# Four graph layers on one core: half of a diagonal block by transposition, row work on ScalarE, shared pair buffers

## Chip, core and metric

The kernel runs on one core of one Trainium2 chip. The metric is the device time of one execution in microseconds (us); several executions are timed and their median is given. The engines are TensorE (PE, matmuls; PEld is its weight load), VectorE (DVE), ScalarE (ACT), GpSimd (POOL) and SyncE (SP), which issues the large transfers. [...]

## What is computed

There are 4096 nodes with 64 features each, `x` (4096 x 64), and one dense matrix `adj` (4096 x 4096). About one entry in 256 of `adj` is nonzero, but the kernel treats it as dense. Four layers follow each other; each takes h = relu(layernorm(x)) and adds its result to x:

```
L0: relu((adj @ h) @ W.T + b)
L1: q, k, h1 = lorentz_linear(...)       # three small linear maps, normalised by row
    att = adj * sigmoid(a * (q . k) + b) ; support = att @ h1
    support / sqrt(|inner(support)|)
L2: log_ij = logmap(h_i, h_j)            # needs acosh-like logarithms for all pairs i, j
    agg_i = sum_j adj_ij / deg_i * log_ij ; expmap(agg @ W + b)
L3: rank of each nonzero of a row (running count), weight 2**-(distance from the last), at most 100;
    out = w @ (h @ W) + b
```

Layer 2's pair value depends on a distance that is the same for (i, j) and (j, i). What differs is only the factor `adj_ij` or `adj_ji`.

## The kernel before, in words

Sources stand on the 128 partitions, targets in the free dimension. The targets are cut into 8 blocks of 512 (`W`, `NB`), the sources into 16 groups of 256 (`NG`, two chunks of 128 each, `G = 2`). A tile of work is thus 128 partitions x 2 chunks x 512 targets, that is 128 x 1024, with the matching piece of the transposed `adj` (512 KB) loaded for it by `feed`.

**Order of work.** The kernel is written as many small generators (one for each step of each layer, such as `l1_sigmoids` or `l2_clamps`), each of which yields the engine it needs next and the time from which it can go. `in_turn` (line 702) picks the next step each time by a cost estimate (`Pace`, line 58: estimated durations and one DMA load per 1.45 us) and so fixes every engine's queue when the program is built. Nothing is decided at run time: a wait in a queue holds all that stands behind it on that engine. Work by row (layernorms, small maps, normalisations: 512 rows at a time) runs in `tail` entries started by `follow`; at most two of those are in progress. They, layer 2's transposes and layer 3's counts share two PSUM banks (`spare`, line 331). `after0` to `after3` finish a layer for a block of rows, `before0` to `before3` prepare the next layer for it.

**Layer 0** (`l0_sums`): PE sums `adj` times `h` per target block. The degrees (row sums of `adj`) are added up on DVE in `degree_sums` (line 835) into a `dg` tile; `LEFT` (line 28) names four source groups of each block whose degrees are left for layer 1 (line 802), except for the last block.

**Layer 1** (`l1_atts`, `l1_sigmoids`, `l1_weights`, `l1_sums`): two matmuls give the scores `mm` in a pair tile of PSUM (two such tiles), ACT takes the sigmoid into one of six `sig` buffers (`SIG`), DVE multiplies by `adj`, PE sums. When a block's last sum is done, `after1` and then `before2` run for it: copies and squares on DVE and ACT, small vectors on DVE, a power on POOL, and four transposes through PE whose results ACT copies into `RT`, `LT`, `RB` and `LB`.

**Layer 2** uses the symmetry. Items (`work`, line 943) are taken for target block i and source block j from i on, two items (halves) for each (i, j): 16 diagonal items with i = j, 56 with i < j (`two`). Each item is worked as follows: distances on PE (`l2_dists`), Square on ACT, clamp on DVE, signs on PE (`l2_signs`), Ln and two Exp on ACT (`l2_roots`), `t<-mm,t` on DVE (`l2_coshs`), Ln on ACT, `t<-t,v` on DVE (`l2_pairs`), `w<-t,adj` on DVE (`l2_weights`), a sum on PE. For `two` items the pair values are also turned by eight PE transposes (`l2_turns`), multiplied by a second `adj` tile (`l2_weights2`, `w<-tr,adj`), summed (`l2_sums2`) and gathered in `others`. `in_steps` (line 1156) fixes the relative order of the steps per engine. `v` and `t` have three buffers each in a pool that is opened in `second_part` (line 956), when layer 1's last sum is done and its buffers are closed; `second_part` also loads the Ln/Exp table on ACT and writes `fars` (a constant of layer 3, 128 x 4096) on DVE.

**Layer 3**: a mask on DVE, counts on PE (`l3_counts`: `tr<-...,pick`, a copy `total` on DVE, `tr<-total,spread`, a copy `chunks` on DVE), ranks on PE (`l3_ranks`, two pair tiles), the weight `wt` on ACT, sums on PE (`l3_sum`). `l3_ranks` issues a pair of ranks and then one or two sums that are possible.

In the profile all instructions have the line of the helper that records them (L128), so they are told apart by the names of their tiles.

Of the kernel before, what the change touches and what calls it, by code (L numbers as in the profile page):

```python
# [9 lines left out]
F32 = mybir.dt.float32  # L10
# [3 lines left out]
AF = mybir.ActivationFunctionType  # L14
# [29 lines left out]
EPS = 0.01  # L44
TURN = "PE"
# [12 lines left out]
class Pace:  # L58
# [56 lines left out]
    def load(self, t):  # L115
        self.free["DMA"] = max(self.free["DMA"], self.now) + 1.45
        self.ready[self.name(t)] = self.free["DMA"] + 2.0
# [18 lines left out]
def kernel(ctx: ExitStack, tc: tile.TileContext, a: dict, out: bass.AP):  # L136
# [313 lines left out]
    def before2(ib, st):  # L450
        rb, lb = rbs[slot["now"]], lbs[slot["now"]]
        h = rt("h", [P, CB, D])
        yield from layernorm_relu(ib, h)
        sq = rt("r_sq", [P, CB, D])
        DVE.tensor_mul(sq, h, h)
# [20 lines left out]
        for k in range(2):  # L476
            DVE.tensor_mul(hh[:, :, k, :], h, ic.to_broadcast([P, CB, D]))
        DVE.tensor_copy(HA[:, cs(ib), 0:D], hh[:, :, 0, :])
        l = rt("l2", [P, CB, D])
        DVE.tensor_scalar(l, hh[:, :, 0, :], -2.0 * SC, None, ALU.mult)  # L480
        yield from transposed(hh.rearrange("p c k d -> p c (k d)"), P, RT[:, ws(ib)])

# [83 lines left out]
    def after1(ib, acc, st):  # L566
        e = rows.tile([P, W], F32, tag="e", name="e")
        DVE.tensor_copy(e, acc)
# [13 lines left out]
        if dg is not None:  # L582
            st["dg_free"][ib % 2] = pace.latest
        yield ON_V
        if dg is not None:
            DVE.tensor_add(
                deg[:, cs(ib), :], deg[:, cs(ib), :], ps[:, n : n + CB].unsqueeze(2)
            )
        s = rt("h", [P, CB, D])
        DVE.tensor_copy(s, v)  # L590
        sq = rt("r_sq", [P, CB, D])
        DVE.tensor_mul(sq, s, s)
# [109 lines left out]
    def in_turn(threads):  # L702
# [5 lines left out]
        while waiting or tail:  # L708
            best = None
            for k, entry in enumerate(tail):  # L710
                if k < 2 or entry["evicts"]:
                    need = entry["need"]() if entry["need"] else 0.0
                    if need is None or (entry["on"] == TURN and not spare):
                        continue
                    start = max(entry["at"], pace.free[entry["on"]], need)
                    if best is None or start < best[0]:
                        best = start, entry
            for thread in waiting:
                on, need = thread[1]
                t = need()  # L720
                if t is not None and (best is None or max(t, pace.free[on]) < best[0] - EPS):
                    best = max(t, pace.free[on]), thread
            pace.now, what = best
            if what in tail:
                advance(what)
                continue
            pace.latest = 0.0
            what[1] = next(what[0], None)
            if what[1] is None:
                waiting.remove(what)  # L730
# [58 lines left out]

    early = ExitStack()  # L790
# [10 lines left out]
    def group(layer, ib, g):  # L801
        degree = (g in LEFT and ib < NB - 1) == (layer == 1)
# [97 lines left out]
    def l1_sigmoids():  # L900
        for n, d in enumerate(l1):
# [3 lines left out]
            d["att"] = w01.tile([P, G, W], F32, tag="sig", name="sig", bufs=SIG)  # L905
# [10 lines left out]
    def l1_sums():  # L916
        for pair in pairs:
# [6 lines left out]
            if d["last"]:  # L924
                ib = d["ib"]
                follow(with_mark(2, ib, after1(ib, acc, st), before2(ib, st)), ON_V, evicts=True)
# [18 lines left out]
         "last": j == NB - 1 and s == CB // G - 1, "two": i < j, "left": 1, "at": 0.0}  # L945
        for i in range(NB) for j in range(i, NB) for s in range(CB // G)
    ]
    twos = [d for d in work if d["two"]]

# [6 lines left out]
    def second_part():  # L956
# [12 lines left out]
        log_exp_tables()  # L969
# [4 lines left out]
    def wt(name, **kw):  # L974
        return w2["pool"].tile([P, G, W], F32, tag=name, name=name, **kw)

    def l2_dists():
        for d in work:
# [3 lines left out]
            pair_tile(d)  # L982
            for c in range(G):
                b = slice(c * D, (c + 1) * D)
                PE.matmul(
                    d["ps"][:, c, :], LT[b, d["g"], :], RT[b, ws(d["ib"])],
                    start=True, stop=False,
                )
            for c in range(G):
                b = slice(2 * c * Q, (2 * c + 1) * Q)  # L990
                PE.matmul(
                    d["ps"][:, c, :], LB[b, d["g"], :], RB[b, ws(d["ib"])],
                    start=False, stop=True,
# [3 lines left out]
    def l2_squares():  # L997
        for k, d in enumerate(work):
            yield "ACT", lambda: latest(
                opened.get("second"), d.get("dist"), ago(work, k, 3, "paired")  # L1000
            )
            d["v"] = wt("v", bufs=3)
            ACT.activation(d["v"], d["ps"], AF.Square)
            d["square"] = pace.latest

    def l2_clamps():
        for d in work:
            yield "DVE", lambda: d.get("square")
            DVE.tensor_scalar(d["v"], d["v"], -half, V_MIN, ALU.add, ALU.max)
            d["clamped"] = pace.latest  # L1010

    def l2_signs():
        for d in work:
            yield "PE", lambda: d.get("square")
            for c in range(G):
                b = slice((2 * c + 1) * Q, (2 * c + 1) * Q + 2)
                PE.matmul(
                    d["ps"][:, c, :], LB[b, d["g"], :], RB[b, ws(d["ib"])],
# [4 lines left out]
    def l2_roots():  # L1023
        for k, d in enumerate(work):
            yield "ACT", lambda: latest(
                d.get("clamped"), ago(work, k, 3, "weighed"), ago(work, k, 3, "turned")
            )
            d["t"] = wt("t", bufs=3)
            ACT.activation(d["v"], d["v"], AF.Ln)
            ACT.activation(d["t"], d["v"], AF.Exp, scale=0.5)  # L1030
            d["root"] = pace.latest
            ACT.activation(d["v"], d["v"], AF.Exp, scale=-0.5)
            d["inverse"] = pace.latest

    def l2_coshs():
        for d in work:
            yield "DVE", lambda: latest(d.get("root"), d.get("signed"))
            DVE.scalar_tensor_tensor(d["t"], d["ps"], 0.5 * SC, d["t"], ALU.max, ALU.add)
            d["read"] = pace.latest

    def l2_logs():
        for d in work:
            yield "ACT", lambda: d.get("read")
            ACT.activation(d["t"], d["t"], AF.Ln, scale=2.0 / SC)
            d["log"] = pace.latest

    def l2_pairs():
        for d in work:
            yield "DVE", lambda: latest(d.get("log"), d.get("inverse"))
            DVE.scalar_tensor_tensor(d["t"], d["t"], top, d["v"], ALU.min, ALU.mult)  # L1050
            d["paired"] = pace.latest

    def l2_weights():
        for k, d in enumerate(work):
            yield "DVE", lambda: latest(d.get("paired"), arrival(d), ago(work, k, 2, "summed"))
            d["w"] = wt("w")
            DVE.tensor_mul(d["w"], d["t"], d["adj"])
# [3 lines left out]
    def l2_turns():  # L1061
        for d in work:
            for c in range(G if d["two"] else 0):
                yield "PE", lambda: d.get("paired") if spare else None
                d["tr", c] = ps = bank()
                for k in range(CB):
                    b = slice(k * P, (k + 1) * P)
                    PE.transpose(ps[:, b], d["t"][:, c, b], ident)
            d["turned"] = pace.latest
            if not d["two"]:  # L1070
# [17 lines left out]
    def l2_weights2():  # L1088
        for k, d in enumerate(twos):
            for c in range(G):  # L1090
# [177 lines left out]
    def l3_ranks():  # L1268


        for n, pair in enumerate(pairs3):
            yield "PE", lambda: latest(
                ready(pair[0]["chunks"]) if "chunks" in pair[0] else None, pair_tiles_free(),
                work[-1].get("dist"),
            )
            chunks = []
            for d in pair:
                pair_tile(d)
                for c in range(G):
                    chunks.append((d["g"] * G + c, d["ps"][:, c, :]))  # L1280
                    PE.matmul(
                        d["ps"][:, c, :], near, d["m"][:, c, :], start=True,
                        stop=chunks[-1][0] == NC - 1, skip_group_check=True,
                    )
            for q, (c, rank) in enumerate(chunks):
                b = slice(q * Q, (q + 1) * Q)
                if c < NC - 1:
                    PE.matmul(
                        rank, late["fars"][b, c, :], pair[0]["chunks"][b, :], start=False,
                        stop=True, skip_group_check=True,  # L1290
                    )
            for d in pair:
                d["ranked"] = pace.latest
            for _ in range(1 + n % 2):
                t = sum_need()
                if sums3 and t is not None:
# [30 lines left out]
    def l3_sum():  # L1327
# [22 lines left out]
        if d["last"]:  # L1350
# [5 lines left out]
        feed(order, "early"), feed(order23, "second"), second_part(), third_part(), l2_loads2(),  # L1356
# [8 lines left out]
            (l2_coshs(), 0, once), (l2_weights2(), 1, if_two(2)),  # L1365
        ),
        l2_gathers(), l3_weights(), l3_ranks(), l3_counts(), l3_masks(),
# [47 lines left out]
```

## Time and profile before

| | |
|---|---|
| three runs | 1213.37, 1216.04, 1216.13 us; median 1216.04 |
| profiled execution | 1215.13 us, its span 1213.4 us, 15538 instructions |
| busy | PE 1085.3 (89%), DVE 980.9 (81%), ACT 797.6 (66%), POOL 114.7 (9%) |
| mean granted PE clock | 0.971 |
| adj transfers | 512 of 512 KB, 271.75 MB in all, mean 224 GB/s |

The rows of the page read: engine, operation, output<-inputs, shape, count | busy us in total, mean ns of one | idle time of that engine just before, and what ended it. Stretches of the span are given from its start.

### The profile page before, as it was taken

The numbers are of one execution on the slowest core, as the hardware profiler recorded it, in microseconds if no ns is written. First come the engines' busy times: TensorE is split into PE (matmuls) and PEld (weight loads), VectorE is DVE, ScalarE is ACT, GpSimd is POOL, SyncE is SP. The second block draws the span as 40 slices with busy tenths as digits, with TensorE's granted clock in tenths as the row PEclk, the third lists the DMA queues.
The fourth block names the chain that finished last, engine by engine and source line by source line (L and its number), as shares of the span: only waits on it lengthen the run. The fifth ranks groups of instructions, "written<-read, shape, count | busy, mean of one in ns | idle before, by whom it ended". The sixth has DMA issues, their size and how long they took to land.

```text
span 1213.4 us, 15538 instructions
## 1 busy us (share of the span) xinstructions
PE 1085.3 (89%) x5368; PEld 443.9 (37%) x5368; DVE 980.9 (81%) x1621; ACT 797.6 (66%) x1204; POOL 114.7 (9%) x99
## 2 busy tenths in 40 slices
PE   4799999998999999689989979989888779999998
PEld 1244443333333333234434434444333323333333
DVE  6788789879999998779989999999989984554551
ACT  1055546666656666589898888888877775555554
POOL 2222212101101010000010010000100120000000
PEclk9899999999999999799999999989989899999999
DMA  8899999864767765335534534444444489888830
GB/s 300 326 393 373 366 362 331 328 234 141 266 227 242 250 230 181 122 120 191 178 125 160 197 105 168 145 139 156 140 156 156 144 311 361 305 306 305 300 110 9
DMA packets 77190, 271.75 MB, mean 224 GB/s; under 512 B 10040, under 2 KB 11064, under 8 KB 77112
## 3 DMA queue, kind: packets, MB, share of 16 engines
q1 hardware_dynamic: 75456, 270.57, 62.7%
q8 instruction: 42, 0.69, 0.2%
q10 hardware_dynamic: 1656, 0.20, 0.1%
q14 instruction: 36, 0.29, 0.1%
HBM read 269.68 MB, written 1.05 MB: 223 GB/s over the span
## 4 chain that ended last, share of the span: by engine, by line
PE 48%; DVE 24%; ACT 13%; issue 7%; DMA 5%; POOL 3%; ACTq 0%; SPq 0%; DVEq 0%; POOLq 0%
PE acc L128 25%; PE mm L128 15%; PE tr L128 9%; DMA adj<-in_adjT_dram 4%; DVE w L128 4%; DVE t L128 4%; ACT wt L128 4%; DVE dg L128 3%; DVE sig L128 2%; ACT v L128 2%; ACT sig L128 2%; POOL lo_s L128 2%; ACT t L128 1%; ACT lo_sq L128 1%; DVE v L128 1%
## 5 line engine op out<-in xcount | busy, mean ns | idle before, releaser
L128 PE MATMUL acc<-w,HA 128*65 128x256 f32 (+1 forms) x736 | 258.6, 488 | 20.9 <-DVE w L128 11.7
L128 ACT ACTIVATE sig<-mm,att_b,att_a 128x1024 f32<-128x1024 f32 x128 | 148.4, 1200 | 83.6 <-PE mm L128 74.8
L128 ACT ACTIVATE v<-v 128x1024 f32<-128x1024 f32 x144 | 152.1, 1057 | 47.6 <-DVE v L128 45.0
L128 ACT ACTIVATE wt<-mm 128x1024 uint16<-128x1024 f32 x124 | 120.2, 1021 | 96.1 <-PE mm L128 96.1
L128 DVE TENSOR_TENSOR sig<-sig,adj 128x1024 f32<-128x1024 f32 x128 | 151.9, 1220 | 11.1 <-ACT sig L128 10.8
L128 PE MATMUL acc<-adj,HA 128*64 128x512 f32 x512 | 127.7, 629 | 23.2 <-DVE HA L128 22.4
L128 DVE TENSOR_TENSOR dg<-dg,adj 128x1024 f32<-128x1024 f32 x113 | 137.9, 1221 | 3.4 <-DMA adj<-in_adjT_dram 2.1
L128 PE MATMUL mm<-qT,kT 64*128 64x512 f32 x512 | 131.7, 623 | 8.8 <-ACT sig L128 8.6
L128 PEld LDWEIGHTS acc<-w,HA 128*65 128x65 f32 x736 | 96.8, 142 | 112.2 <-issue 64.6
L128 PE MATMUL acc<-sig,HL 128*64 128x512 f32 x512 | 122.5, 603 | 0.8 <-DVE sig L128 0.8
L128 PE MATMUL acc<-wt,S 128*64 128x512 bf16 x496 | 99.6, 390 | 0.2 <-ACT wt L128 0.2
L128 DVE SCALAR_TENSOR_TENSOR t<-t,v 128x1024 f32<-128x1024 f32 x72 | 89.7, 1246 | 9.8 <-ACT t L128 9.8
L128 DVE SCALAR_TENSOR_TENSOR t<-mm,t 128x1024 f32<-128x1024 f32 x72 | 87.6, 1217 | 4.5 <-PE mm L128 4.2
L128 PE MATMUL mm<-RT,LT 64*128 64x512 f32 x288 | 82.6, 651 | 7.2 <-DVE t L128 7.0
L128 DVE TENSOR_TENSOR w<-t,adj 128x1024 f32<-128x1024 f32 x72 | 87.8, 1220 | 1.4
L128 ACT ACTIVATE t<-t 128x1024 f32<-128x1024 f32 x72 | 75.5, 1049 | 9.4 <-DVE t L128 9.4
L128 DVE TENSOR_TENSOR w<-tr,adj 128x512 f32<-128x512 f32 x112 | 73.2, 684 | 9.9 <-PE tr L128 9.9
L128 DVE TENSOR_SCALAR RT<-adj 128x1024 bf16<-128x1024 f32 x74 | 49.7, 690 | 37.0 <-PE mm L128 36.5
L128 ACT ACTIVATE t<-v 128x1024 f32<-128x1024 f32 x72 | 76.1, 1057 | 2.3
L128 PEld LDWEIGHTS mm<-qT,kT 64*128 64x128 f32 x512 | 42.4, 185 | 86.1 <-ACT sig L128 49.0
L128 ACT ACTIVATE v<-mm 128x1024 f32<-128x1024 f32 x72 | 72.6, 1008 | 1.6 <-PE acc L128 1.6
L128 PE MATMUL tr<-ident,t 128*128 128x128 f32 x448 | 61.0, 279 | 7.7 <-DVE t L128 4.4
(201 smaller groups left out, 1301.3 us busy)
## 6 DMA issues: line engine op xcount, KB each, us to landing
adj<-in_adjT_dram SPq DMA_DIRECT2D x512, 512.0 KB, 4.7
x<-in_x_dram SPq DMA_DIRECT2D x4, 256.0 KB, 4.1
out_dram<-h SPq DMA_DIRECT2D x8, 128.0 KB, 2.9
b<-in_b_dram ACTq DMA_DIRECT2D x2, 32.0 KB, 6.5
W<-in_W_dram ACTq DMA_DIRECT2D x3, 16.0 KB, 4.0
W0T<-in_W0T_dram ACTq DMA_DIRECT2D x2, 16.0 KB, 5.4
W1T<-in_W1T_dram ACTq DMA_DIRECT2D x1, 16.0 KB, 5.2
W1T<-in_b_dram ACTq DMA_DIRECT2D x1, 0.2 KB
```

The lines of the kernel that those rows point to most:

```text
L128: done = self.tc.keep_in_program_order(getattr(self.engine, op)(*args, **kw))
```

## The change

- **Cut items.** The second item of each diagonal block (`cut`) is worked only for the block's last 256 targets; all its steps run on 128 x 2 x 256. For its first 256 targets, the pair values of the first item (sources 0 to 255, targets 256 to 511) are turned by four PE transposes in a spare bank and multiplied by `adj` in one more DVE instruction.
- **Rows on ScalarE.** In `after1` and `before2` the copies, squares and scalings of one operand go from DVE to ACT: `e`, `h`, two `r_sq`, the second half of `r` (`hh`), the copy to `HA`, `l`; a small copy `r_c` is new.
- **Pair buffers.** One pool of six buffers serves `sig` in layer 1 and `v` and `t` in layer 2. The first squares need only the buffers of layer 1's older groups, not the end of layer 1. The table load is put right after layer 1's last sigmoid (`second_tables`).
- **Rows wait at the hand-over.** From the table load until item 4 (`FIRST`) is weighed, `in_turn` sets the row steps back by 0.02 us of planned time, so that layer 2's own steps go first where both could.
- **Degrees.** Block 0's four left degree groups go back to layer 0.
- **Layer 3.** While a pair of ranks can't be issued in the plan, sums that can are issued ahead of it (`l3_pass`).
- **Planner.** A load is planned at 1.37 us, not 1.45.

```diff
     def load(self, t):
-        self.free["DMA"] = max(self.free["DMA"], self.now) + 1.45
+        self.free["DMA"] = max(self.free["DMA"], self.now) + 1.37
...
     (before2)
+        yield ON_S
         sq = rt("r_sq", [P, CB, D])
-        DVE.tensor_mul(sq, h, h)
+        ACT.activation(sq, h, AF.Square)
+        yield ON_V
...
-        for k in range(2):
-            DVE.tensor_mul(hh[:, :, k, :], h, ic.to_broadcast([P, CB, D]))
-        DVE.tensor_copy(HA[:, cs(ib), 0:D], hh[:, :, 0, :])
+        DVE.tensor_mul(hh[:, :, 0, :], h, ic.to_broadcast([P, CB, D]))
+        yield ON_S
+        ACT.copy(hh[:, :, 1, :], hh[:, :, 0, :])
+        ACT.copy(HA[:, cs(ib), 0:D], hh[:, :, 0, :])
         l = rt("l2", [P, CB, D])
-        DVE.tensor_scalar(l, hh[:, :, 0, :], -2.0 * SC, None, ALU.mult)
+        ACT.activation(l, hh[:, :, 0, :], AF.Copy, scale=-2.0 * SC)
...
     (after1)
-        DVE.tensor_copy(e, acc)
+        ACT.copy(e, acc)
...
+        yield ON_S
+        s = rt("h", [P, CB, D])
+        ACT.copy(s, v)
+        sq = rt("r_sq", [P, CB, D])
+        ACT.activation(sq, v, AF.Square)
...
     (in_turn)
+                    if "tables" in opened and "weighed" not in work[FIRST]:
+                        start += 2 * EPS
...
+    pairp = ctx.enter_context(tc.tile_pool(name="pairs", bufs=SIG))
+    def pair_buffer(name):
+        return pairp.tile([P, G, W], F32, tag="pair", name=name)
...
-        degree = (g in LEFT and ib < NB - 1) == (layer == 1)
+        degree = (g in LEFT and 0 < ib < NB - 1) == (layer == 1)
...
+    OWN = G * P
+    def part(d, t):
+        return t[:, :, OWN:] if d["cut"] else t
+    def targets(d):
+        return slice(d["ib"] * W + (OWN if d["cut"] else 0), (d["ib"] + 1) * W)
...
+    def second_tables():
+        yield "ACT", lambda: l1[-1].get("read")
+        log_exp_tables()
+        opened["tables"] = pace.free["ACT"]
...
     (l2_squares)
-                opened.get("second"), d.get("dist"), ago(work, k, 3, "paired")
+                d.get("dist"), l1[2 * k - SIG].get("summed") if 2 * k < SIG else 0.0,
+                ago(work, k, SIG // 2, "paired"),
...
     (l2_turns)
+            if d["first"]:
+                yield "PE", lambda: d.get("paired") if spare else None
+                d["tr", 0] = ps = bank()
+                for k in range(CB):
+                    b, c = slice(OWN + k // G * P, OWN + (k // G + 1) * P), k % G
+                    PE.transpose(ps[:, k * P : (k + 1) * P], d["t"][:, c, b], ident)
...
     (l2_weights2)
+                own["w"] = w2["pool"].tile([P, G, W], F32, tag="w", name="w")
+                DVE.tensor_mul(
+                    own["w"][:, :, 0:OWN], d["tr", 0].rearrange("p (k j) -> p k j", j=OWN),
+                    own["adj"][:, :, 0:OWN],
+                )
...
     (l3_pass, was l3_ranks)
+            while rank_need(pair) is None:
+                yield "PE", lambda: first_of(rank_need(pair), sum_need() if sums3 else None)
+                if rank_need(pair) is None:
+                    l3_sum()
+            yield "PE", lambda: rank_need(pair)
+            l3_rank(pair)
```

## Prediction

> **What bounds the kernel now.** I read the page's engine shares first (PE 89%, DVE 81%, ACT 66%). Those are means over four layers, so I cut the span into stretches. The columns are length, then busy time (and instructions) of PE, PEld, DVE, ACT and POOL, granted clock, DMA share and GB/s:
>
> ```profile
> 0.00:50.00 50.00, 27.56 (x95) 7.77 (x96) 33.80 (x82) 5.30 (x11) 13.21 (x35) 0.90 0.82 303
> 50.00:230.00 180.00, 171.48 (x889) 73.72 (x890) 156.99 (x239) 94.68 (x321) 42.07 (x22) 1.00 0.97 368
> 230.00:487.00 257.00, 244.25 (x1112) 88.44 (x1108) 229.19 (x475) 162.31 (x284) 26.89 (x16) 1.00 0.66 222
> 487.00:532.00 45.00, 29.68 (x116) 11.44 (x112) 31.66 (x66) 28.54 (x45) 2.32 (x2) 0.77 0.27 94
> 532.00:605.00 73.00, 72.89 (x345) 34.94 (x344) 68.47 (x78) 66.55 (x70) 0.00 (x0) 1.00 0.54 182
> 605.00:975.00 370.00, 324.11 (x1468) 150.88 (x1466) 343.86 (x488) 309.23 (x336) 24.11 (x19) 0.95 0.44 149
> 975.00:1004.00 29.00, 23.05 (x130) 7.98 (x130) 24.56 (x56) 20.72 (x28) 6.08 (x5) 0.94 0.94 355
> 1004.00:1206.00 202.00, 189.23 (x1214) 67.15 (x1210) 91.23 (x141) 109.58 (x114) 0.00 (x0) 1.00 0.68 248
> ```
>
> To be seen: layer 0 (to 230) runs at DMA's rate with a nearly full PE; layer 1 (230 to 487) at PE's; at 487 to 532 no engine is full, that is the hand-over to layer 2; layer 2's plain stretch (532 to 605) is PE's, 5.85 us an item, with 0.4 us of DVE slack in each; 605 to 975 holds the diagonal blocks and rows, PE loses 46 us and DVE is nearly gapless; layer 3 is PE's, with 12.8 us lost.
>
> Second, the timeline around 487, where the hand-over is lost:
>
> ```profile
> 486.50 1.23 DVE L128 TENSOR_TENSOR sig<-sig,adj 128x1024 f32<-128x1024 f32 x1 [1.43 <-ACT sig L128]
> 491.20 1.02 ACT L128 ACTIVATE v<-mm 128x1024 f32<-128x1024 f32 x1 [1.58 <-PE acc L128]
> 496.76 1.06 ACT L128 ACTIVATE v<-v 128x1024 f32<-128x1024 f32 x1 [4.54 <-DVE v L128]
> 500.70 2.08 PE L128 MATMUL mm<-RT,LT 64*128 64x512 f32 x4 [7.01 <-DVE t L128]
> 507.53 3.68 PE L128 MATMUL acc<-w,HA 128*65 128x512 f32 x4 [4.20 <-DVE w L128]
> 530.93 1.23 DVE L128 TENSOR_TENSOR w<-t,adj 128x1024 f32<-128x1024 f32 x1
> ```
>
> The first square of layer 2 waits until layer 1's last sum is done (its buffers lie where layer 1's lay); then its clamp stands in DVE's queue behind `fars` and block 7's rows. The last line is the weighing of item 3. Third, groups by form and waits, for prices:
>
> ```profile
> L128 DVE SCALAR_TENSOR_TENSOR t<-mm,t 128x1024 f32<-128x1024 f32 x72 | 87.6, 1217 | 4.5 <-PE mm L128 4.2 <-ACT t L128 0.2
> L128 DVE TENSOR_TENSOR w<-tr,adj 128x512 f32<-128x512 f32 x112 | 73.2, 684 | 9.9 <-PE tr L128 9.9
> L128 DVE TENSOR_SCALAR v<-v 128x1024 f32<-128x1024 f32 x72 | 49.3, 684 | 2.3 <-ACT v L128 2.3
> PE mm L128 <- ACT sig L128: 8.6, 17, 1.2
> PE tr L128 <- DVE total L128: 6.1, 8, 0.8
> PE mm L128 <- ACT wt L128: 3.4, 13, 0.3
> ```
>
> The last three are layer 1's and layer 3's PE waits (total, times, longest).
>
> **The change, part by part.** All sums are against the profiled execution: 1215.1 us, its span 1213.4.
>
> *Cut items.* Eight second diagonal items become half as wide. Off DVE, each: clamp 0.68 to about 0.35, cosh and pair product 1.22 and 1.25 to 0.68 each (the 512-wide row). The weighing of 1.22 becomes two of 0.68. Net 3.15+1.22 against 1.71+1.36: 1.3 us saved. ACT saves five times 0.43 (1.057 to 0.63, on the line between 0.414 at 256 wide, `r_sq<-ln_xc`, and 1.057 at 1024), 2.1 us. PE saves about half a `mm<-RT,LT` group (0.5 us of 1.13) and pays four transposes (0.6): nothing. The new wait: the second weighing waits for those transposes and a spare bank; behind it on DVE stand the next clamp and pair product. The nearest row, `w<-tr`, waited 9.9 us over 29 of 112, 0.1 us each; at most the 0.4 us of its worst. For the seven blocks in the DVE-bound stretch 605 to 1000: 7 x 1.3 = 9, of which I take 8, because six times (10.8 us) PE waited there for `ACT v`. Ends 4 and 10.
>
> *Rows on ScalarE.* Per block off DVE (start to start, block 7's timeline): `e` 0.61, `h` 0.45, two `r_sq` 0.91, second `r` 0.34, `HA` and `l` 0.20 each: 2.7 us. On to ACT: 0.58 + 0.37 + 2 x 0.41 + 3 x 0.40 + 0.2, about 3.2 us. [...] (`S<-hb` 0.399 on ACT, `HA<-r` 0.28, 0.20 start to start, on DVE). Counted in engine time the move loses 0.5 us a block, 4 us. Counted by what bounds, it pays: in layer 1 ACT has 95 us idle of 257.
>
> In layer 1, seven blocks x 2.7 and the degree sums of block 0 (copy, three adds, half add: 4.6) take some 23 us off DVE. PE is the bound there and can gain no more than its idle 12.8. DVE is gapless from 267 to 310, and in 275 to 300 PE loses 4.3. Elsewhere PE is sent two score groups in a row because weights are late, and waits for a pair tile (8.6 in 17 waits). In the changed program's order such doubles fall from 17 to 10: 8.6 x 7/17 = 3.5, partly the same time as the 4.3. I take 5; ends 1 and 8.
>
> *Degree sums into layer 0.* Four adds of 1.22, 4.9 us of DVE before 50, where it has 16 us idle; they stand ahead of the half add of `dg` (44.4, now about 49.5), which PE's transposes need at 49.7. The order puts two more `acc<-adj` matmuls ahead of them. If DVE's room fails, four buffers come free later and DMA-bound layer 0 slips. I take 0; ends -1 (gain) and +2.
>
> *Hand-over.* In the changed program the first square follows the last sigmoid on ACT, its clamp the last `sig` product on DVE; `fars` follows, rows come after item 3. From the shown anchor (last `sig` product ending 487.7): square ends 487.5; clamp 488.4; `fars` 490.6; the table load (1.28 in the trace) ends about 489; Ln and two Exp to 492.3; cosh 492.5; Ln 493.8; pair product 495.1; first weights 496.3, against 507.5. Item 1 is half, its weights done by 499.4; item 2 about 505.7; item 3 at 510.8 against 532.1. That is 21 us earlier, but before had done block 7's rows by then. Those now cost DVE 12.5 - 2.7, some 9.5 us, among items with 0.4 us slack each, so over six items 7 us come back. ACT holds 3.2 + 4.7 us of row work there against 0.75 slack an item. I allow 3 more for ACT standing in its queue for PE (`LB` waited 4.19 at 528). 21 - 7 - 3 = 11; ends 5 and 14.
>
> The clock: in the trace the 7.0 us PE gap is followed by a group at 2.08 instead of 1.13 and sums at 3.68 instead of 1.93. [...] by the row alone a shorter gap might keep the clock and give some 2 us more. [...] no gain from the clock, inside the upper end.
>
> *Table load.* Earlier by its place in the queue, same number (19); counted above. [...] The trace has 488.33 + 1.28, nothing following, so I keep 1.28.
>
> *Layer 3.* A sum may now go while ranks wait. In the old order 9 of 16 `tr<-total` groups follow directly on counting (`pick`) and wait for its copy, in the new 13 of 16 follow a sum of 1.5 us, longer than the 0.8 it hides. So the 6.1 go, 5.5 to be careful; the 3.4 stay. Ends 2 and 7.
>
> *At no cost:* the pair buffers in layer 2 (three `v` and three `t` as before, strictly in turn), the planner's load price and delay of rows (order only).
>
> Sum: 5 + 11 + 8 + 5.5 + 0 = 29.5. 1215.1 - 29.5 = 1185.6, say 1186; the runs' median of 1216.0 is 0.9 above the profiled one, which is within their spread, so it is left.
>
> **The rivals.** (a) *The hand-over only shifts the rows* (0.25). DVE, ACT and PE are all near 5.1 to 5.85 us an item, so 9.5 us of deferred rows come back in full and queueing eats more: 5 there, 2 in layer 1, 6 at the diagonals, 5 in layer 3: 18, 1197. For it: ACT is 91% busy in 532 to 605. Against: before idles DVE 13 us here.
> (b) *Everything lands at its good end* (0.15): 8 + 13 + 9 + 6 = 36 and up, 1178. For it: DVE's gaplessness at 900 to 1000, where each us saved is a us.
> (c) *Slower* (0.03): ScalarE's in-order queue. Each block has gained four round trips between DVE, ACT and PE; if row copies wait there for transposes as `LB` did (4.19, with DVE's `t` idle 4.82 behind it), all five activations stand. It decides from 29.5 / 8 = 3.7 us a block; at 4.5 it costs 36: 1222. Against: ACT's rows waits in layer 1 sum to 17 us over seven blocks, and PE did not wait on most.
> (d) *It does not do what it says* (0.02): halves cost what wholes do and rows only move: within 0.3%, 1215. The 512-wide rows speak against it.
>
> **Numbers.** Main case 0.55 at 1186, 1181 to 1192. The range takes (a) and (b) with their spread: 1175 to 1201. A measurement tells about 0.3% apart; faster by more 0.95, within 0.02, slower 0.03.
>
> **What will show it.** First `acc<-w` some 6 us after the end of layer 1's last sum instead of 16; item 3 weighed near 21 us earlier against that sum; `PE tr <- DVE total` near 1; half-wide `v`, `t` forms at 0.35, 0.68 and 0.63; layer 1's `PE mm <- ACT sig` about 5. Wrong if ACT waits for PE transposes by several us a block, or if 605 to 975 keeps its length because PE, not DVE, sets it.

## The result and the profile after

The changed kernel takes 1198.38 us (median of four runs, 1195.06 to 1202.06), the kernel before 1214.7 in the same comparison: 0.986 of the time, with a 95% interval of 0.983 to 0.988. The forecast was 1186 with a range of 1175 to 1201. The time lies in the range, near rival (a)'s 1197 and not in the main case: some 16 to 19 us were gained where 29.5 were summed. Rival (a)'s total is met and its terms are not (5, 2, 6 and 5 for hand-over, layer 1, diagonals and layer 3, against 9.0, 4.7, 4.3 and 0.9 in the table below), so that the total came out near it is luck.

The profiled execution after took 1196.08 us, span 1194.4, clock 0.978: 19.0 less than the profiled one before. I cut it near the same places of the work (columns: length, then busy time and instructions of PE, PEld, DVE, ACT, POOL, granted clock, DMA share, GB/s):

```profile
230.00:483.00 253.00, 247.04 (x1106) 88.78 (x1104) 208.41 (x421) 178.31 (x336) 25.47 (x16) 0.99 0.68 225
483.00:510.00 27.00, 21.34 (x88) 7.90 (x87) 20.56 (x28) 24.43 (x30) 0.95 (x1) 0.87 0.48 164
986.00:1189.00 203.00, 190.59 (x1195) 69.33 (x1215) 92.31 (x143) 111.84 (x117) 0.00 (x0) 1.00 0.68 246
```

The hand-over row (the second) is 27 us where it was 45, but the block's rows are now behind it. The stretch to dwell on is the one with the diagonal blocks. From the end of the 16th weighing (`w<-t,adj`, the last of the first block row) to layer 2's last sum, before (first line) and after:

```profile
600.64:977.08 376.44, 330.40 (x1492) 153.49 (x1489) 349.77 (x498) 314.58 (x340) 24.11 (x19) 0.95 0.44 149
586.89:959.00 372.11, 325.99 (x1518) 153.90 (x1517) 340.69 (x500) 297.77 (x338) 26.20 (x18) 0.97 0.44 150
```

DVE has lost 9.1 us of work, as sized (7 x 1.3), and the stretch only 4.3. From milestone to milestone of the two traces:

| stretch | before | after | gain | forecast |
|---|---|---|---|---|
| start to the end of the last `sig` product | 487.73 | 483.04 | 4.7 | 5 |
| from there to the 16th `w<-t,adj` (the first block row) | 112.9 | 103.9 | 9.0 | 11 |
| from there to layer 2's last sum | 376.5 | 372.1 | 4.3 | 8 |
| from there to layer 3's last sum | 231.1 | 230.1 | 0.9 | 5.5 |

The timeline of the hand-over in the changed kernel shows that part as it was drawn up. The columns are start, length, engine, operation, and in brackets the idle time before and its releaser:

```profile
481.81 1.23 DVE L129 TENSOR_TENSOR sig<-sig,adj 128x1024 f32<-128x1024 f32 x1 [1.43 <-ACT sig L129]
482.55 1.02 ACT L129 ACTIVATE v<-mm 128x1024 f32<-128x1024 f32 x1 [0.77 <-PE mm L129]
483.61 0.69 DVE L129 TENSOR_SCALAR v<-v 128x1024 f32<-128x1024 f32 x1 [0.56 <-ACT v L129]
489.50 2.08 PE L129 MATMUL mm<-RT,LT 64*128 64x512 f32 x4 [3.62 <-DVE t L129]
493.07 3.44 PE L129 MATMUL acc<-w,HA 128*65 128x512 f32 x4
```

The first square comes 0.8 us after the last sigmoid, the first sum starts 7.2 us after layer 1's last one ended (485.89) where it took 16, and the first groups still run slow after a gap of 3.62 us (2.08 us for 1.13, at a granted clock of 0.50 from 489.33 to 496.16). The small forms cost near what they were priced at (the clamp 0.42, for 0.35), and PE's waits named in the prediction went down or away:

```profile
L129 DVE SCALAR_TENSOR_TENSOR t<-t,v 128x512 f32<-128x512 f32 x8 | 5.5, 682 | 0.0
L129 ACT ACTIVATE v<-v 128x512 f32<-128x512 f32 x16 | 10.1, 630 | 9.8 <-DVE v L129 9.5
L129 DVE TENSOR_SCALAR v<-v 128x512 f32<-128x512 f32 x8 | 3.3, 415 | 0.0
PE mm L129 <- ACT sig L129: 3.3, 8, 0.7
```

Of `PE tr <- DVE total` (6.1) one wait of 0.5 is left. So the prices held; what failed is how much of them became time.

### The profile page after: what moved, and what is told of

The parts are those of the page before. It is cut to its first block, busy times and chain, and to the rows that moved or that the text cites. A ratio compares the mean times of both kernels' runs of the same rounds, so it can differ in the third digit from the quotient of the medians.

```text
span 1194.4 us, 15545 instructions
## 1 busy us (share of the span) xinstructions
PE 1077.9 (90%) x5367; PEld 445.8 (37%) x5392; DVE 950.6 (80%) x1571; ACT 800.7 (67%) x1266; POOL 118.2 (10%) x99
## 4 chain that ended last, share of the span: by engine, by line
PE 47%; DVE 25%; ACT 13%; issue 7%; DMA 5%; POOL 2%; SPq 0%; ACTq 0%; DVEq 0%; POOLq 0%
PE acc L129 23%; PE mm L129 16%; PE tr L129 8%; DVE t L129 6%; DVE w L129 6%; DVE dg L129 4%; DMA adj<-in_adjT_dram 4%; ACT wt L129 3%; ACT v L129 3%; ACT t L129 2%; DVE v L129 1%; DVE sig L129 1%; POOL lo_s L129 1%; ACT sig L129 1%; ACT lo_sq L129 1%
## 5 line engine op out<-in xcount | busy, mean ns | idle before, releaser
L129 PE MATMUL acc<-w,HA 128*65 128x256 f32 (+1 forms) x736 | 252.6, 479 | 22.2 <-DVE w L129 13.8
L129 ACT ACTIVATE v<-v 128x1024 f32<-128x1024 f32 (+1 forms) x144 | 145.3, 1009 | 54.5 <-DVE v L129 52.2
L129 PE MATMUL acc<-wt,S 128*128 128x512 bf16 (+1 forms) x480 | 98.7, 391 | 2.7 <-issue 2.4
L129 DVE SCALAR_TENSOR_TENSOR t<-t,v 128x1024 f32<-128x1024 f32 x72 | 85.4, 1186 | 5.2 <-ACT t L129 5.2
L129 DVE SCALAR_TENSOR_TENSOR t<-mm,t 128x1024 f32<-128x1024 f32 x72 | 83.3, 1157 | 4.1 <-ACT t L129 2.1
L129 DVE TENSOR_TENSOR w<-tr,adj 128x512 f32<-128x512 f32 x120 | 78.5, 683 | 10.1 <-PE tr L129 10.1
L129 DVE TENSOR_TENSOR w<-t,adj 128x1024 f32<-128x1024 f32 x72 | 83.5, 1160 | 1.2
L129 PE MATMUL tr<-ident,t 128*128 128x128 f32 x480 | 67.7, 283 | 16.7 <-DVE w L129 6.9
L129 PE MATMUL mm<-RT,LT 64*128 64x512 f32 (+1 forms) x288 | 78.9, 625 | 3.6 <-DVE t L129 3.6
L129 ACT ACTIVATE t<-t 128x1024 f32<-128x1024 f32 x72 | 72.1, 1002 | 13.3 <-DVE t L129 13.2
```

Source lines behind the costliest of these rows:

```text
L129: done = self.tc.keep_in_program_order(getattr(self.engine, op)(*args, **kw))
```

## The experiments

Since the planner fixes all queues anew for each kernel, the runs are read by the same milestones as above, next to their medians. "Boundary" is the time from the weighing before a new block row of layer 2 to the sixth after it; boundaries 1 to 4 are alike in content. Lengths in us:

| kernel | boundaries 1, 2, 3, 4 | median | ratio to before, 95% interval |
|---|---|---|---|
| before | 40.85, 40.90, 42.28, 41.99 | 1216.04 | |
| before, second trace | 40.84, 41.73, 42.29, 40.88 | 1214.77 | 0.9993 [0.9978, 1.0008] |
| changed | 40.49, 40.54, 40.54, 40.54 | 1198.38 | 0.9857 [0.9833, 0.9882] |
| no cut | 42.23, 42.06, 42.28, 42.03 | 1206.06 | 0.9926 [0.9900, 0.9953] |
| rows on DVE | 40.49, 40.54, 40.54, 40.54 | 1208.61 | 0.9936 [0.9919, 0.9953] |
| old layer 3 | 40.70, 40.55, 40.54, 41.08 | 1201.52 | 0.9873 [0.9845, 0.9902] |
| old hand-over | 40.50, 40.55, 40.54, 40.55 | 1200.39 | 0.9862 [0.9842, 0.9883] |
| tanh by exponentials | 40.02, 40.08, 40.07, 40.08 | 1195.77 | 0.9831 [0.9812, 0.9851] |
| rows last | 34.42, 40.53, 34.55, 41.40 | 1212.19 | 0.9958 [0.9944, 0.9972] |
| both of these | 34.49, 39.11, 44.28, 45.34 | 1223.26 | 1.0055 [1.0032, 1.0078] |
| clamp first | 39.78, 43.71, 42.48, 40.79 | 1207.18 | 0.9935 [0.9911, 0.9959] |
| idle PE work, no cut | 42.66, 40.95, 40.95, 40.97 | 1202.42 | 0.9897 [0.9869, 0.9925] |
| one sum per rank pair | 40.76, 40.54, 40.82, 41.00 | 1200.45 | 0.9867 [0.9845, 0.9888] |
| rows only | 40.84, 41.61, 42.29, 41.80 | 1207.69 | 0.9939 [0.9918, 0.9959] |

### One part undone at a time

**No cut.** All items whole, and the steps for the cut items left out:

```diff
-         "two": i < j, "cut": i == j and s == 1,
-         "left": 1 + (i == j and s == 1), "at": 0.0}
+         "two": i < j, "cut": False,
+         "left": 1, "at": 0.0}
```

> The changed kernel with whole second diagonal items (no cut); all else as changed. Theory A (the cut saves DVE the 1.3 us a block that was sized, but at a block boundary most of it turns into waits in the chain of DVE, ScalarE and TensorE that makes the next block's rows, so it is worth what the traces differ by): 4 to 5 us slower than the changed kernel (some 1200.5 in the trace), the stretch from the 16th to the last weighing of the first half longer by 3 to 5. Rival B (the cut is worth its full 8 to 9, and another part, the rows on ScalarE, costs 4 in the same stretch): 8 to 9 slower, 1204 to 1205.

Slower than the changed kernel by 0.0069 of the time before, 8.4 us (about ±4.5, the half widths of the two intervals put together; so below too). The stretch from the 16th to the last weighing is 377.7 instead of 370.1: 7.5 longer, all of it at the boundaries. Layer 3, counted from layer 2's last sum, is 2.3 shorter; its first output comes after 40.0 us, where the changed kernel takes 41.5. By its numbers this is rival B; but B's cause, rows on ScalarE, is gone with the next run. The 8.4 also holds an accident of the new order, at 562, before the first boundary:

```profile
562.34 0.57 ACT L129 COPY others<-acc 65x512 f32<-65x512 f32 x1
562.96 3.40 PE L129 MATMUL acc<-w,HA 128*65 128x256 f32 x8 [6.22 <-ACT others L129]
```

PE waited 6.2 us for a copy that stood behind rows' and items' work in ScalarE's queue, and then ran its sums slow (3.40 us for 1.94). That cost has nothing to do with the cut as such. It comes again, 6.2 us, in the other kernel without the cut (idle PE work, below), so it belongs to this order and not to one execution. With it the 16th weighing comes 111.4 us after the last `sig` product; kernels with the cut and the same order ahead of it have 103.9 to 105.9. So the 8.4 overstates the cut: in this trace it is worth 7.5 less layer 3's 2.3 behind the first block row, and the 7.5 owes much to the clock, as is shown below. The accident is rival (c)'s mechanism, seen at last, in a kernel that differs by one part.

**Rows on DVE.** `e`, `h`, both `r_sq`, the second half of `r`, `HA` and `l` as before:

```diff
-        ACT.activation(sq, h, AF.Square)
+        DVE.tensor_mul(sq, h, h)
...
-        ACT.copy(e, acc)
+        DVE.tensor_copy(e, acc)
...
```

> The changed kernel with the rows' one-operand work of layers 1 and 2 back on VectorE; all else as changed. Theory A: slower by 5 to 10 (layer 1 loses its 4 to 5, the rows of block 7 cost VectorE 2.7 more at the hand-over, each boundary of layer 2 loses some 0.5 to 1). Rival B (rows on ScalarE take back 4 us of what the cut saves at the diagonals): the stretch from the 16th to the last weighing gets shorter by 3 to 4, layer 1 and hand-over longer by 5, and the whole within 2 us of the changed kernel.

Slower by 0.0079, 9.6 us (about ±3.7). Layer 1 (last `acc<-adj` to last `sig` product) is 276.9 instead of 274.5, the hand-over 112.0 instead of 103.9 (4.5 of that is again PE waiting for `others<-acc` on ScalarE), and the diagonal stretch is the same to 0.1 us: 370.2 and 370.1. So A in the main, though layer 1's 2.4 lie within its scatter (see below) and the 0.5 to 1 that A had for each boundary did not come; and B falls: the rows moved are made in layer 1 and at the hand-over, and do nothing at the later boundaries. With the 4.5, not all of the 9.6 is the rows' own price.

**Old layer 3.** `l3_ranks()` in place of `l3_pass()`.

> The changed kernel with layer 3's old order of ranks and sums; all else as changed. Theory A (the new order saves the 0.64 us a block by which the period of layer 3's blocks fell, 28.28 to 27.64, and gives 2.6 back in the last block, where sums ran ahead and two pairs of ranks stand without one between): slower by 1 to 2, the last block short again (near 24.8). Rival B (the order is worth the 5.5 that was forecast, and the start of layer 3 has lost 4 through the other parts): slower by 5.

From layer 2's last sum to layer 3's last: 231.9 instead of 230.1, so the order is worth 1.8 in the trace, as theory A had it; the medians are 0.0016 apart, 1.9 ±4.6, which agrees and could not tell alone. The last block takes 24.8 again, the others 28.28.

**Old hand-over.** Own buffers for `v` and `t`, table load and first square after layer 1's last sum, rows not held back:

```diff
     (pair_buffer)
-        return pairp.tile([P, G, W], F32, tag="pair", name=name)
+        return w2["pool"].tile([P, G, W], F32, tag=name, name=name, bufs=3)
...
+        log_exp_tables()
         opened["second"] = l1[-1]["summed"]
```

> The changed kernel with layer 2's own buffers for v and t again, its table load and first squares after layer 1's last sum, and block 7's rows not held back; cut, rows on ScalarE and layer 3's order stay. Theory A: slower by 8 to 10, all of it before the 16th weighing; the first weighing some 16 us after the end of layer 1's last sum. Rival B (the early start only moves the rows, which come back later in full): slower by 3 to 5.

Slower by 0.0005: 0.6 us (about ±3.9). In its trace the third item after the first is weighed 33.3 us after the last `sig` product instead of 27.0, but the 16th 106.1 after it instead of 103.9. Both theories said more; B, that the early start only moves the rows, is the nearer.

### Where the hand-over's gain comes from

**Rows only.** The kernel before with the rows' work on ScalarE (and the degree sums and the planner's price), nothing else.

> The kernel before with only the rows' work on ScalarE, the degree sums of block 0 in layer 0 and the planner's load price: no cut, layer 2's own buffers, layer 3's old order. Theory A (the hand-over's gain is largely VectorE's 2.7 us less for block 7's rows and their shorter queue, not the early first square, whose undoing cost 2.2): from the last sig product to the 16th weighing some 106 us (112.9 before, 103.9 after), the whole 5 to 9 faster than before. Rival (rows alone are worth nothing at the hand-over, where VectorE idled 13 us): 111 to 113, the whole 1 to 4 faster.

The whole is 7.4 us (about ±2.5) faster than before, as A had it. By the medians the rows are as large a part of the change as any, alone (7.4) as well as undone (9.6).

From the last `sig` product to the 16th weighing it takes 107.9. So the rows alone bring 5.0 of the 9.0 there; with the cut and the new layer 3 (the old hand-over's run) it is 106.1; with the early start it is 103.9 in the changed kernel's trace, but 105.6 to 105.9 in the four others whose DVE and ScalarE queues are the same up to there (one sum per rank pair, old layer 3, tanh, clamp first). The difference is the clock: behind the gap of 3.62 us each of these four has a second stretch at half clock (20 or 64 to 65 us after the last `sig` product), and falls back by about 2 us there; the changed kernel's trace has none. The early square is worth 0 to 2 us.

### What holds the boundaries

**The kernel before, traced again.**

> The kernel before, unchanged, traced a second time. Two of its block boundaries (1 and 2) took 40.9 us in the first trace and the next two 42.3 and 42.0, with the same instructions in the same order up to a group acc<-w that ran at half speed in the last two (3.2 us for 1.93). Theory C (whether TensorE's clock falls at that place varies from execution to execution; it costs 1.3 to 1.4 each time): boundaries again at either 40.9 or 42.0 to 42.3, not in the same pattern, and each long one has the slow acc<-w group. Rival D (something in the program makes 3 and 4 longer): the same pattern, 40.9, 40.9, 42.3, 42.0. It also shows how far the end of layer 0 moves with no change to the code (217.3 us in the first trace; 208 to 215 in the variants of the changed kernel).

Theory C. Boundary 2 was 40.90 and is 41.73, boundary 4 was 41.99 and is 40.88, in one program, in which DVE and ScalarE execute the same instructions in the same order both times. Boundary 2 in the first trace:

```profile
700.70 0.63 PE L128 MATMUL tr<-ident,l 128*64 128x128 f32 x4 [2.00 <-DVE l L128]
701.83 1.93 PE L128 MATMUL acc<-w,HA 128*65 128x512 f32 x4 [0.51 <-DVE w L128]
```

and in the second:

```profile
701.35 1.06 PE L128 MATMUL tr<-ident,l 128*64 128x128 f32 x4 [1.99 <-DVE l L128]
702.48 3.06 PE L128 MATMUL acc<-w,HA 128*65 128x512 f32 x4
```

The same wait for DVE's `l`, then the same transposes and the same sum at full or at half speed. The granted clock falls at 701.38 in the second trace, as the transposes start. The falls lie on a grid. In the first trace stretches at half clock begin at 631.89, 778.66, 795.73 and 843.51, which are 43, 5 and 14 times 3.413 us apart, and in this trace and in the changed kernel's all thirteen of each begin on such a grid, whose position differs between the two. They last 3.41 us or a multiple of it (the last one runs into the end). On its own grid, the first trace (first two lines) and the second (columns as above):

```profile
696.75:700.16 3.41, 1.95 (x10) 0.40 (x8) 3.31 (x9) 2.51 (x4) 0.00 (x0) 1.00 0.20 80
700.16:703.57 3.41, 2.36 (x8) 1.02 (x9) 3.32 (x5) 2.90 (x4) 0.00 (x0) 1.00 0.24 47
697.97:701.38 3.41, 1.42 (x10) 0.36 (x10) 3.27 (x9) 2.84 (x3) 0.00 (x0) 1.00 0.05 22
701.38:704.79 3.41, 3.34 (x7) 1.25 (x8) 2.89 (x4) 2.90 (x5) 0.00 (x0) 0.50 0.34 107
```

In the first the wait is divided between two stretches of the grid (PE busy 1.95 and 2.36), in the second it lies in one (1.42), and the next stretch runs at half clock. At boundaries 1 to 4 of the four traces without the cut (before twice, no cut, rows only) it is so sixteen times: the clock falls around this wait in eleven, and these are the eleven that take 41.6 to 42.3; the other five take 40.84 to 40.90. Where it falls in the two traces of before, PE was busy for 0.93 to 1.42 us of the stretch before, where it does not, for 1.64 or more in each. (Elsewhere the clock also falls behind a fuller stretch, as in the changed kernel at 380.10 with 3.09 us of PE work in the 3.41 us before, so this is no rule for other work.)

The distances of the next item stand behind the sum on PE; where it is slow, DVE's next `t<-mm,t` comes 0.8 to 1.4 us later. The changed kernel's boundary 2 has no such gap:

```profile
683.79 0.60 PE L129 MATMUL tr<-ident,l 128*64 128x128 f32 x4 [0.52 <-DVE l L129]
684.32 1.13 PE L129 MATMUL mm<-RT,LT 64*128 64x512 f32 x4
686.10 1.93 PE L129 MATMUL acc<-w,HA 128*65 128x512 f32 x4 [0.33 <-DVE w L129]
```

There the clock falls, where it does, in a turned sum later in the boundary (3.31 us for 1.94 at 611.8 in boundary 1), and the boundary is 40.5 all the same. Where it falls there for twice as long (6.8 us: boundaries 1 and 4 of old layer 3; 1, 3 and 4 of one sum per rank pair), the boundary takes 40.7 to 41.1.

**Idle PE work in the kernel without the cut.** Ten transposes of `ident` that nobody reads:

```diff
+            if warm(d):
+                yield "PE", lambda: 0.0 if spare else None
+                ps = bank()
+                for k in range(WARM):
+                    b = slice(k % CB * P, (k % CB + 1) * P)
+                    PE.transpose(ps[:, b], ident, ident)
+                emptied(ps)
```

> The changed kernel without the cut, plus ten idle transposes of 0.13 us on TensorE at each of the six later block boundaries, ahead of the gap of 2.0 us in which it waits for VectorE's l; their result is read by nobody. Theory C (the long boundaries are long because the clock falls in that gap): boundaries 1 to 4, 42.0 to 42.3 without the idle work, become 40.7 to 41.2, and their acc<-w groups 1.9 us. Rival (those boundaries are long from VectorE's 1.3 us of added work alone): the same 42 or longer by the added work.

Boundaries 2 to 4 become 40.95, 40.95 and 40.97 as C has it, boundary 1 does not (42.66; why was not followed up). The planner also put the sum behind the next transposes (`tr<-W,columns`), so two things changed; at boundary 3 the sum is still slow (2.64) and the boundary is short. This run fits C but doesn't prove it; the two traces of the kernel before do. From the 16th to the last weighing it takes 371.4, where the cut takes 370.1 and the same kernel without the idle work 377.7: in these traces work that nobody reads is worth nearly as much there as the cut. The whole has the accident of the no-cut order in it, and its interval overlaps with that of no cut, so a gain in time is not shown.

**Tanh by exponentials.** The same function by another formula, without the two table loads at each boundary:

```diff
-        ACT.activation(th, n[:, 0:CB, :], AF.Tanh)
-        log_exp_tables()
+        ACT.activation(th, n[:, 0:CB, :], AF.Exp, scale=2.0)
         yield ON_V
+        DVE.tensor_scalar(th, th, 1.0, None, ALU.add)
+        DVE.reciprocal(th, th)
+        DVE.tensor_scalar(th, th, -2.0, 1.0, ALU.mult, ALU.add)
```

> The changed kernel, with the row scale's tanh worked out as 1 - 2/(exp(2n)+1), so that the two table loads of 1.28 us at each block boundary of layer 2 go; three small VectorE operations of 0.17 us more. Theory A (at a boundary the cut has moved the limit from VectorE to ScalarE: it stands idle 2.3 us for a clamp queued behind row work, then runs gapless for some 13 us through both loads while VectorE waits for it): each of boundaries 1 to 4, 40.5 us now from the weighing before to the sixth after, becomes 1 to 2 shorter, the whole 5 to 10 us. Rival B (VectorE's own work sets the boundary also after the cut): boundaries 0 to 0.5 longer, the whole 0 to 3 slower.

Each boundary is 0.47 shorter, with 0.4 us more of DVE's work in it: a gain, but neither theory's. Of the 2.5 us that ScalarE is spared a fifth becomes time. It has the lowest median of all kernels here; its interval and the changed kernel's overlap, so it is not shown to be faster.

**Row steps last.** `"weighed" not in work[-1]` in place of `work[FIRST]`.

> The changed kernel, where the planner puts a row step of layer 2 behind an item's step that could start at the same moment, up to the last weighing instead of only up to item 4. Only the order changes. Theory A (at a boundary row work ahead of the next clamp starves ScalarE, which costs the cut its gain): clamp directly after its square, ScalarE's 2.3 us wait gone, boundaries 1 to 2 shorter each. Block 7's rows are spread over more items: each item of layer 2's first block has 0.4 us of VectorE to spare, so the payback of 8 us between items 3 and 10 shrinks by 1 to 4. In all 5 to 12 faster. Rival B (the boundary is a sum of work of VectorE, whatever its order): boundaries the same within 0.3, the whole within 2 us.

Slower, where both theories had it faster or the same. From the 16th to the last weighing it gains 3.4 us (366.7): boundaries 1 and 3 take 34.4 and 34.6, with 4 to 5 us less of DVE's work in them. But this row work comes back, and it is what layer 3 needs: layer 2's last sum ends 9.6 us after the last weighing, where it was 2.0, and from there to layer 3's first output it takes 48.5 us, where the changed kernel takes 41.5.

**Both.**

> Both: tanh by exponentials, and row steps behind item steps to the end of layer 2. Theory A: the two relieve the same ScalarE stretch in part, so less than their sum: boundaries 2 to 3 shorter each than the changed kernel, 10 to 15 us in all. Rival B (VectorE's work sets the boundary): no faster than the row order alone.

Slower than the kernel before; both theories missed. The boundaries run together, and PE waits up to 4.9 us for `e` at single ones. Row order matters more than any one price here.

**Clamp first.** Rows held back 1 us of planned time between the cut item's clamp and the next one:

```diff
+                    if clamp_due():
+                        start += HOLD
```

> The changed kernel, where at boundaries 1 to 6 the planner holds row steps back by 1 us between the clamp of the cut item and that of the item after it; only the order changes. Theory A (that clamp stands behind row work on VectorE, ScalarE starves 2.3 us and VectorE later waits 1.2 for the next square): boundaries 1 to 4 at 39.3 to 40.0 instead of 40.5. Rival B (VectorE's own work and the rows' chain set them, any order): 40.3 to 40.8.

At boundary 1 it does what A says: 39.78. At boundaries 2 and 3 the row steps come late, PE waits 2.0 us for `columns`, its sum runs slow (3.62 and 3.37 us for 1.93), and they take 43.7 and 42.5. Inconclusive as a whole.

### Layer 3's last block

**One sum per rank pair in the last block.**

```diff
-                yield "PE", lambda: first_of(rank_need(pair), sum_need() if sums3 else None)
+                yield "PE", lambda: first_of(rank_need(pair), sum_need() if sums3 and n < len(pairs3) - 8 else None)
...
-            for _ in range(1 + n % 2):
+            for _ in range(1 + n % 2 if n < len(pairs3) - 8 else 1):
```

> The changed kernel, except that in the last of layer 3's eight blocks a sum goes only after each pair of ranks, none while counts are awaited. Theory A (the reordered sums run ahead, and in the last block, where no later work refills them, two rank pairs stand without a sum between them and TensorE waits 1.5 us for ScalarE): last block, 27.4 us from the seventh output to the eighth, becomes 1 to 1.5 shorter. Rival B (the last block is longer only because TensorE's own work was shifted into it from the blocks before): within 0.3.

The last block falls from 27.4 to 25.0, the one before it rises from 27.6 to 29.0: 1.0 us in all. Both theories were partly right: of 2.4 us, 1.4 was work shifted between two blocks, 1.0 real waiting. In the medians (1200.45 and 1198.38, with intervals that overlap) it does not show.

## Why the gain was forecast too high

**Layer 1: right within its ends.** Forecast 5 (1 to 8); one trace says 4.7. The end of layer 0 moves by 6 us with the same code (208.1 to 214.6 in the variants), so one trace can't carry that. Over eleven traces with this layer 1 (all variants but rows on DVE, and the changed kernel) the last `sig` product ends at 484.6 on average (480.5 to 489.0), in two traces of before at 488.1: 3.5. PE's wait for `sig` in the layer fell from 8.6 to 2.9, below the 5 that I named. The two layers also share the time differently (layer 0 ends 8.8 earlier in the trace, layer 1 is 4.1 longer); why was not followed up. So the size is right, and that it came from the cause named is not shown: the rows put back on DVE made layer 1 2.4 longer, and the same layer 1 takes 271.2 to 276.2 in the eleven traces.

**Hand-over: size right within its ends, cause wrong.** The step "That is 21 us earlier ... 21 - 7 - 3 = 11" put the gain on the early first square. Counted from the last `sig` product, item 3 is weighed 17.4 us earlier (27.0 instead of 44.4), not 21, and at the twelfth weighing the lead is down to 9.1. A payback of that kind was foreseen. But with the early start undone nearly all of the gain stays, and rows on ScalarE alone bring 5.0: what counts is above all where block 7's rows are worked, not when layer 2 starts. Rival (a) had this as "only shifts the rows", at 5. That the clock would bring nothing was the author's estimate; the first groups are slow again (2.08 and 3.44 us after the gap of 3.62). The clock was not worth nothing, though: about 2 of the 9.0 are the second stretch at half clock that this one execution was spared, which is luck. The other four traces of this order gain 7.0 to 7.3.

**Diagonals: the step that failed.** "For the seven blocks in the DVE-bound stretch: 7 x 1.3 = 9, of which I take 8". DVE lost what was sized; here are boundary 2 before and after, both at full clock:

```profile
688.57:729.47 40.90, 32.73 (x154) 14.77 (x153) 37.89 (x58) 35.58 (x40) 3.35 (x3) 1.00 0.39 129
```

```profile
674.47:715.01 40.54, 33.23 (x156) 14.83 (x155) 36.61 (x59) 33.45 (x40) 4.19 (x3) 1.00 0.38 130
```

DVE's busy time fell by 1.28, the boundary by 0.36. The other 0.9 is new idle time of DVE, 3.0 before and 3.9 after. Its place, in the timeline of the changed kernel:

```profile
679.02 1.01 ACT L129 ACTIVATE v<-mm 128x1024 f32<-128x1024 f32 x1
...
683.56 0.68 DVE L129 TENSOR_SCALAR v<-v 128x1024 f32<-128x1024 f32 x1
...
684.28 1.06 ACT L129 ACTIVATE v<-v 128x1024 f32<-128x1024 f32 x1 [2.29 <-DVE v L129]
...
687.89 1.02 ACT L129 ACTIVATE v<-mm 128x1024 f32<-128x1024 f32 x1
688.93 0.69 DVE L129 TENSOR_SCALAR v<-v 128x1024 f32<-128x1024 f32 x1 [1.25 <-ACT v L129]
```

The square of the item after the cut one is done at 680.0, its clamp runs at 683.6 behind row work, ScalarE stands 2.3 us and is then behind, and DVE waits 1.25 for the following square. That `DVE v <- ACT v` was 0.3 in boundary 2 before and is 1.5 after. That this wait is what ate the 0.9 is read from the trace; moving the clamp forward bore it out at boundary 1 only (39.8), and elsewhere other waits came in its place. Taking ScalarE's table loads away moved it by 0.5.

The rest of the gain there is not DVE's work at all. At boundaries 1 to 4 the four traces without the cut average 41.7, the changed kernel's 40.5. Of this 1.15, only 0.35 is left between boundaries where no sum on the path ran slow (40.85 to 40.9 against 40.5). The other 0.8 is the clock: without the cut PE waits 1.3 us (boundary 1) or 2.0 for `l`, and its clock fell in 11 of those 16 boundaries; with the cut it waits 0.4 to 0.5 and, in the changed kernel's trace, the fall comes where nothing hangs on it. I had set the clock at nothing here. In the two traces that the prediction is measured by, before's clock fell at boundaries 3 and 4 and not at 1 and 2: the gains are 0.35, 0.35, 1.7 and 1.5, then 0.9 at the fifth boundary, and the last is 0.5 longer. That makes 4.3 of the 8; which of before's boundaries were hit is luck, so another pair of traces would give another sum.

**Layer 3: mechanism right, size wrong.** "So the 6.1 go, 5.5 to be careful". They went, and others came. Blocks 4 to 7 of the changed kernel, total, times, longest:

```profile
PE acc L129 <- issue: 1.3, 8, 0.2
...
PE tr L129 <- DVE RT L129: 1.3, 2, 0.6
...
PE tr L129 <- DVE LT L129: 0.6, 1, 0.6
PE tr L129 <- DVE RB L129: 0.6, 1, 0.6
```

In the same four blocks of before PE waited 3.2 for `total` and 2.1 for `wt`: 5.3 us went, these 3.8 came. (That leaves 1.5 of the 2.6 us that four periods gained; the rest is not accounted for.) The counts that no longer wait for a copy now wait for the masks, which lie in the tiles `RT`, `LT` and `RB` here: I did not ask what is late next. The period of a block fell by 0.64, from 28.28 to 27.64. The first block gained 1.6, five periods 3.2, the last lost 2.6 because its sums had been done ahead, and the start lost 1.3 (layer 3's first output comes 41.5 us after layer 2's last sum, in the two traces of before 40.3 and 40.7): 0.9. The loss at the start seems to go with the cut: it is there in the kernels that have the cut and the same row order, with the old layer 3 as well (41.1 to 41.6), and not in the two changed kernels without it (40.0 and 39.6). Why was not followed up.

**Degree sums, table load: no cost seen.** Layer 0 ended earlier in all other traces than in before's two (217.3 and 216.4); the load took 1.28 and Ln followed it at 485.15, as forecast from the trace of before. What the degree sums alone do can't be told under layer 0's 6 us of scatter.

**What stays open.** Whether another order of the boundary's steps turns all of the cut's 1.28 into time; three orders were tried, each won at one place and lost at another.

## What to carry to other kernels

An engine that is 93% busy in a stretch is not yet the bound of it: cut its work in one place and see, instruction by instruction, who is late next, before multiplying a saving by the number of blocks. Where a planner fixes the queues, undoing one flag reorders the rest, so compare milestones and not only totals, and look for the accident (here a copy of 0.57 us that cost 6). Trace the unchanged kernel twice: the second trace told a fall of the clock from a property of the program. And count a part's gain over several traces: here 2 us of one part's 9 and most of another's were the clock.

## What was not expected of the hardware

TensorE's clock fell behind a wait of 2.0 us, with PE at work before and after it: the stretch of 3.41 us ahead of the fall held 1.17 and 1.41 us of PE work at boundaries 3 and 4 of the first trace of before. With the same instructions it fell in one execution and not in the next: `acc<-w` took 1.93 and 3.06 us at the same place of the same program. The same wait of 2.0 us cost nothing where it was divided between two stretches of the grid of 3.413 us (1.95 and 2.36 us of PE work in them), and was followed by a fall where it lay in one (1.42). What a fall cost differed with what stood behind it: at the turned sum nothing, or 0.2 to 0.6 us where it lasted 6.8 us; at the sum ahead of the next distances 0.8 to 1.4 us.

Layer 0's end moved between 208.1 and 214.6 us in the twelve traces other than before's, although DVE and ScalarE have the same instructions in the same order there. That is more than most parts of this change are worth.
